# Places for the experts' tokens: 48 tiles of 256 slots and 9 of 128, with the second bias scaled by ScalarE

## The chip, the core and the metric

The program runs on one core of one Trainium2 chip. The metric is the device time of one execution in microseconds. The kernel before was run three times: 1418.8 us is the median, 1416.08 and 1422.6 us are the ends.

## What is computed

The input is an image of two pictures, 56 x 56 positions and 256 channels each, so 6272 tokens. Layer 0 adds a neighbourhood attention (windows of 7 x 7, eight heads). Layer 1 adds a gated linear attention over the tokens in order, and then a mixture of experts, which is the part that the change touches:

```python
xf = _ln_t(t).reshape(-1, 256)                      # 6272 tokens
probs = softmax(xf @ gate_w + gate_b)               # 8 experts
top2_vals, top2_idx = top_k(probs, 2)
cw = zeros((N, 8)).at[arange(N)[:, None], top2_idx].add(top2_vals)
for e in range(8):                                  # W1: 256 x 512, W2: 512 x 256
    h = gelu(xf @ W1[e] + b1[e])
    out += cw[:, e:e+1] * (h @ W2[e] + b2[e])
```

Each token goes to two of the eight experts, so there are 12,544 pairs of token and expert. Everything is float32.

## The kernel before, in words

**Layer 0** (`attend`, `scores`, `context`) comes first. **Layer 1** then walks over 13 steps of 256 positions in both pictures; `before(s)` makes keys, values, queries and coefficients, `attention(s)` the attention itself, and `route(s)` (L1188) the gate of the experts. The order in which these generators are written out is interleaved by hand in `together` (L1517); the framework's scheduler then orders the instructions of each engine, and each engine runs its own in order.

**Routing.** Every expert has a region of rows in the DRAM tensor `xs_d`. `route(s)` counts the tokens of each expert, and writes each normalised token with its index and its weights into the next free row of its two experts, with indirect DMAs that GpSimd issues (L1287, "puts"). `listed(s)` (L1304) keeps a list of tiles: each tile of `SL` = 256 consecutive rows of one expert that is full by now gets the next entry (first row in `l_row`, expert in `l_exp`). After the last step, `listed(NS1)` adds the one partly filled tile that an expert may have at its end. There are `NX` = 56 places in all: 6272 x 2 pairs fill at most that many tiles of 256. A place whose tile doesn't exist points at a spare region. Places 0 to 40 are sure to be known after step 11, place 41 after step 12, and places 42 to 55 after `listed(NS1)`. Before that, eight DMAs on SyncE's queue (L1597) write 256 blank rows behind each expert's last token, so that the unfilled slots of a last tile are harmless.

**Experts.** For each place `k` in order, `experts` (L1493) does this:
- `fetch(k)` (L1369), on SyncE's queue: it loads row and expert into registers, and starts a DMA for the 256 token rows `xg` (272 KB, L1382) and one for the expert's weights `wj` (1154 KB, L1391). A fetch waits for the puts whose rows it reads. Weights and tokens have eight buffers in the last part, where the pool `tw` joins `fw`.
- `gather(k)` (L1394): VectorE takes the token numbers `rowk` and the weights of this expert `cws` out of `xg`; TensorE turns the tokens with four transposes (`pt_g`, L1419) and ScalarE copies them to `xT_g`; GpSimd writes `ye` = second bias times weight, twice 128 x 256 (L1426).
- `hidden(k)` (L1429): eight matmuls (`p_h`, L1436; each float32 matmul runs as two instructions) with 256 moving columns, and four activations with Gelu on ScalarE (L1443).
- `results(k)` (L1447): for each half `u` of 128 slots, four matmuls (`p_y`, L1456), then VectorE adds `p_y` times weight to `ye` (L1463), and GpSimd issues an indirect DMA that adds the 128 rows of `ye` to the rows of `out` (L1466, "adds"). Each add of a tile waits until both adds of the tile before have landed, since two experts can have the same token. `ye` has four buffers (pool `fy`).

`gather(k + 1)` is written out ahead of `results(k)`. In the walk over the steps, expert tiles run beside attention as far as they are known: 39 of them (places 0 to 38) are done when step 12 is routed. The other 17 (places 39 to 55) follow in a last part with nothing beside them, which in the profile begins at 1258.95 us on TensorE.

Of the kernel before, what the change touches and what calls it, by code (L numbers as in the profile page):

```python
# [66 lines left out]
FW = 4  # L67


def size(s):  # L70
    W = min(B1, L - s * B1)
    T = min(P, W)
    return W, T, W // T

# [696 lines left out]
def layer1(tc, t, out, x1_d, xs_d, ident, load, K, plain, lx, last_row, lite):  # L771
# [12 lines left out]
    with ExitStack() as whole:  # L784
# [519 lines left out]
        def listed(s):  # L1304
            last = s == NS1
            lo, hi = sure1(s - 1), NX if last else most1(s)
# [3 lines left out]
            if last:  # L1310
                nc.vector.scalar_tensor_tensor(new, c_prev, float(SL), n_prev, ALU.mult, ALU.is_lt)
# [8 lines left out]
            if hi > lo:  # L1320
# [14 lines left out]
                wide = [P, hi - lo, 2 * NE]  # L1335
                hit = p1.tile(wide, F32, tag="hit", name="hit")
                nc.vector.tensor_tensor(
                    hit,
                    K.c_pos[:, lo:hi].unsqueeze(2).to_broadcast(wide),
                    pos.rearrange("p e i -> p (e i)").unsqueeze(1).to_broadcast(wide),  # L1340
                    ALU.is_equal,
                )
                val = p1.tile(wide, F32, tag="val", name="val")
                add = p1.tile([P, hi - lo], F32, tag="add", name="add")
                for what, of in ((K.l_row, row), (K.l_exp, K.c_exp)):
                    nc.vector.tensor_tensor(
                        val,
                        hit,
                        of.rearrange("p e i -> p (e i)").unsqueeze(1).to_broadcast(wide),
                        ALU.mult,  # L1350
                    )
                    nc.vector.tensor_reduce(add, val, AX.X, ALU.add)
                    nc.vector.tensor_add(what[:, lo:hi], what[:, lo:hi], add)
            state["c"] = c
            known = len(entry)
            now = NX if last else sure1(s)
            if now > known:
                ent = entries.tile([1, 2, NX], I32, tag="ent", name="ent")
                nc.vector.tensor_copy(ent[:, 0, known:now], K.l_row[0:1, known:now])
                nc.vector.tensor_copy(ent[:, 1, known:now], K.l_exp[0:1, known:now])  # L1360
                entry.extend([ent] * (now - known))

        entry, added, puts, stores = [], [], {}, {}
        fetched = {}

        def filled_at(k):
            return next((s for s in range(NS1) if sure1(s) > k), NS1)

        def fetch(k, pool):  # L1369
            known = "the lists hold rows of the regions and experts alone"  # L1370
            row, exp = (
                nc.values_load(
                    entry[k][0:1, n, k : k + 1],
# [5 lines left out]
                for n, top in ((0, NE * RG), (1, NE - 1))  # L1379
# [3 lines left out]
                out=xg, in_=xs_d[bass.ds(row, SL), :].rearrange("(u p) c -> p u c", p=P)  # L1383
# [10 lines left out]
        def gather(k, pool, psum):  # L1394
            xg, wj = fetched[k]
            rowk = fs.tile([P, SL // P], I32, tag="rowk", name="rowk")
            tc.keep_in_program_order(
                nc.vector.tensor_scalar(
                    rowk, xg[:, :, TOK].bitcast(I32), 0.0, float(NB * L + SL - 1), ALU.max, ALU.min
# [4 lines left out]
            for u in range(SL // P):  # L1404
# [4 lines left out]
                        K.l_exp[:, k : k + 1],  # L1409
# [7 lines left out]
            for u in range(SL // P):  # L1417
                for g in range(NG):
                    nc.tensor.transpose(  # L1419
                        pt[:, g, u * P : (u + 1) * P], xg[:, u, g * P : (g + 1) * P], ident  # L1420
                    )
            xT = pool.tile([P, NG, SL], F32, tag="xT_g", name="xT_g")
            nc.scalar.copy(xT, pt)
            y = fy.tile([P, SL // P, C], F32, tag="ye", name="ye")
            for u in range(SL // P):
                nc.gpsimd.tensor_scalar_mul(y[:, u, :], wj[:, WJ - C :], cws[:, u : u + 1])  # L1426
            return xT, cws, rowk, y

        def hidden(xT, wj, pool, psum):  # L1429
            w1 = wj[:, : NG * FF].rearrange("p (k f) -> p k f", k=NG)  # L1430
            b1 = wj[:, NG * FF + NF * C : NG * FF + NF * C + NF]
            hT = pool.tile([P, NF, SL], F32, tag="hT", name="hT")
            for f in range(NF):
                ph = psum.tile([P, SL], F32, tag="mm", name="p_h")
# [12 lines left out]
        def results(k, hT, made, wj, pool, psum):  # L1447
            xT, cws, rowk, y = made
# [4 lines left out]
            for u in range(SL // P):  # L1453
# [27 lines left out]
                if u == 0:  # L1481
                    yield
# [4 lines left out]
        def ask(k):  # L1487
            while use.asked < min(k, NX):
                n = use.asked
                fetch(n, use.w if use.tail is None or (n - use.tail) // FW % 2 else tw)  # L1490
                use.asked += 1

        def experts():  # L1493
            for k in range(NX):
# [6 lines left out]
                if k + 1 < NX:  # L1501
# [83 lines left out]
        behind_ = p1.tile([P, NE], I32, tag="behind", name="behind")  # L1585
# [3 lines left out]
        for e in range(NE):  # L1589
            row = nc.values_load(  # L1590
                behind_[0:1, e : e + 1],
                engines=[mybir.EngineType.SP],
                min_val=e * RG,
                max_val=e * RG + NB * L,
                skip_runtime_bounds_check_because="an expert has at most K.every token",
            )
            put = nc.sync.dma_start(  # L1597
                out=xs_d[bass.ds(row, SL), :].rearrange("(u p) c -> p u c", p=P), in_=empty
            )
            tc.declare_no_dep(put.ins, group="puts", reason="slots behind the last token")  # L1600
# [916 lines left out]
```

## Time and profile before

| what | value |
|---|---|
| time, median of 3 | 1418.8 us |
| time of the profiled execution | 1421.03 us |
| its span in the profile | 1419.2 us |
| granted TensorE clock, mean | 0.938 |
| busy: TensorE, VectorE, GpSimd, ScalarE | 90%, 56%, 41%, 39% |
| adds L1466: number, busy | 112, 179.3 us of GpSimd |
| scalings L1426: number, busy | 112, 126.5 us of GpSimd |
| `p_h` and `p_y` on TensorE | 222.1 us and 214.9 us |
| HBM read and written | 131.55 MB and 50.30 MB |

The span is the time from the first to the last recorded instruction. "Busy" is the time in which an engine ran an instruction; PEld is the loading of weights on TensorE, which runs beside the matmuls. The chain of work that ended last is followed back from the last instruction; it gives one path, and another that is nearly as long doesn't show in it. So the timeline of a single engine has to be read as well, above all GpSimd's, whose queue holds the adds.

### The profile page before, as it was taken

Reading aid. Unit: us, or ns where it says so; the run is one execution under the profiler, and the core shown is the slowest. Engines: PE = TensorE matmul, PEld = TensorE weight load, DVE = VectorE, ACT = ScalarE, POOL = GpSimd, SP = SyncE. Lnnn points to the kernel's source line nnn. Section 1 sums busy time; section 2 is a strip of 40 time slices with the busy share of each in tenths; the row PEclk is TensorE's granted clock in tenths of the full one; section 3 lists DMA queues with packets and bytes.
Section 4 is the critical chain, followed back from the end, with each engine's and each line's share of the span. In section 5 each row is a group of like instructions: output and inputs, shape, how many; then the busy total and the mean of one; then the engine's idle time right before and its main releaser. Section 6 shows DMA issues by size and latency. Waiting matters only on the chain.

```text
span 1419.2 us, 30057 instructions
## 1 busy us (share of the span) xinstructions
PE 1281.3 (90%) x11620; PEld 933.6 (66%) x11620; DVE 799.5 (56%) x2679; ACT 551.3 (39%) x943; POOL 587.9 (41%) x633
## 2 busy tenths in 40 slices
PE   2999989899989997897989999999999999988994
PEld 1567667677845754455666767677676777877883
DVE  6545555565767566767576665657575764331120
ACT  1433434443444232243534445353535344322331
POOL 0222322232321314214172737355554566664774
PEclk9999999999989696887999999999999999999997
DMA  9344454333421011024253536262644546679842
GB/s 290 88 120 144 123 152 123 100 111 113 140 90 40 27 36 62 25 80 151 85 165 93 171 97 202 69 192 83 174 123 125 163 129 195 201 213 373 223 60 34
DMA packets 103036, 183.93 MB, mean 130 GB/s; under 512 B 15666, under 2 KB 86578, under 8 KB 95716
## 3 DMA queue, kind: packets, MB, share of 16 engines
q1 hardware_dynamic: 69844, 128.75, 27.9%
q0 software_dynamic: 29872, 48.12, 14.9%
q10 hardware_dynamic: 3168, 5.05, 1.1%
q8 instruction: 93, 1.52, 0.4%
q14 instruction: 59, 0.48, 0.1%
HBM read 131.55 MB, written 50.30 MB: 128 GB/s over the span
## 4 chain that ended last, share of the span: by engine, by line
PE 49%; DVE 13%; DMA 3%; issue 2%; ACT 2%; POOL 2%; POOLq 0%; DVEq 0%; ACTq 0%
PE p_y L1456 11%; PE p_qkv L917 10%; PE p_h L1436 9%; PE p_out L1170 4%; DMA out<-ye,rowk 3%; PE cx L1152 2%; PE p_u L939 2%; PE cx L1139 2%; PE p_sum L954 2%; PE pt_x L889 2%; DVE am L1101 1%; PE pt_g L1419 1%; PE p_cf L1052 1%; DVE root_a L848 1%; ACT wide L1042 1%
## 5 line engine op out<-in xcount | busy, mean ns | idle before, releaser
L1466 POOL DMA_INDIRECT out<-ye,rowk x112 | 179.3, 1601 | 212.3 <-DMA out<-ye,rowk 44.3
L1436 PE MATMUL p_h<-xT_g,wj 128*128 128x256 f32 x896 | 222.1, 388 | 7.1 <-DVE ye L1463 6.2
L1456 PE MATMUL p_y<-wj,hT 128*128 128x256 f32 x896 | 214.9, 387 | 14.1 <-DVE am L1101 8.0
L1456 PEld LDWEIGHTS p_y<-wj,hT 128*128 128x128 f32 x896 | 166.1, 193 | 43.2 <-DVE am L1101 8.7
L1436 PEld LDWEIGHTS p_h<-xT_g,wj 128*128 128x128 f32 x896 | 163.0, 191 | 34.9 <-DVE ye L1463 6.6
L382 ACT ACTIVATE ex<-ex 98x1024 f32<-98x1024 f32 x98 | 103.6, 1057 | 195.9 <-DVE ex L376 194.6
L1443 ACT ACTIVATE hT<-p_h,wj 128x256 f32<-128x256 f32 x224 | 105.0, 474 | 191.2 <-PE p_h L1436 172.8
L1426 POOL TENSOR_SCALAR ye<-wj,cws 128x256 f32<-128x256 f32 x112 | 126.5, 1309 | 83.4 <-DVE own_e L1406 62.7
L1463 DVE SCALAR_TENSOR_TENSOR ye<-p_y,cws,ye 128x256 f32<-128x256 f32 x112 | 54.0, 482 | 167.9 <-POOL ye L1426 110.4
L376 DVE TENSOR_TENSOR ex<-sc,bias 98x1024 f32<-98x1024 f32 (+1 forms) x112 | 120.2, 1084 | 30.2 <-PE sc L367 27.0
L334 POOL TENSOR_TENSOR xo<-xo,xq 128x256 f32<-128x256 f32 x49 | 36.0, 735 | 225.9 <-DVE xo L328 210.9
L367 PEld LDWEIGHTS sc<-qb,kc 64*98 64x98 f32 x1568 | 94.5, 168 | 51.2 <-issue 27.9
L390 PE MATMUL po<-vw,ex 98*64 98x33 f32 x3136 | 117.6, 230 | 5.0 <-ACT ex L382 2.4
L367 PE MATMUL sc<-qb,kc 64*98 64x128 f32 x1568 | 118.1, 288 | 3.8 <-DVE am L1101 2.2
L390 PEld LDWEIGHTS po<-vw,ex 98*64 98x64 f32 x3136 | 106.2, 144 | 22.8 <-ACT ex L382 4.8
L1287 POOL DMA_INDIRECT xs_d<-xs,rowi x100 | 97.9, 979 | 37.9 <-issue 18.9
L1125 POOL TENSOR_TENSOR zc<-z,blk 128x256 f32<-128x256 f32 x48 | 42.3, 895 | 119.6 <-DVE z L1123 111.6
L494 PE MATMUL pvv<-L_wvT,xs 128*112 128x256 f32 x224 | 60.6, 410 | 14.4 <-DVE top L486 14.4
L1101 DVE TENSOR_TENSOR am<-sc,upto 128x512 f32<-128x512 f32 (+1 forms) x100 | 60.9, 671 | 5.8 <-PE sc L1092 5.8
L336 POOL DMA_DIRECT2D x_d<-xo x98 | 56.6, 579 | 16.6 <-POOL xo L334 14.6
L946 DVE TENSOR_TENSOR pd<-p_u,k 128x512 f32<-128x512 f32 (+1 forms) x26 | 17.2, 661 | 79.1 <-PE pt_gate L1222 64.5
L861 DVE BATCH_NORM_STATS2 st<-x_acc 128x6 f32<-128x256 f32 (+1 forms) x100 | 38.3, 413 | 40.7 <-DMA x_acc<-x_d 40.2
(244 smaller groups left out, 2179.1 us busy)
## 6 DMA issues: line engine op xcount, KB each, us to landing
wj<-in_we SPq DMA_DIRECT2D x56, 1154.0 KB
vw<-v_d SPq DMA_DIRECT2D x196, 101.1 KB
xg<-xs_d SPq DMA_DIRECT2D x56, 272.0 KB
v_d<-values POOLq DMA_DIRECT2D x28, 231.0 KB, 3.2
xq<-in_x SPq DMA_DIRECT2D x98, 64.0 KB
x_d<-xo POOLq DMA_DIRECT2D x98, 64.0 KB, 3.2
x_acc<-x_d SPq DMA_DIRECT2D x24, 256.0 KB
out<-x_acc POOLq DMA_DIRECT2D x24, 256.0 KB, 3.9
```

The lines of the kernel that those rows point to most:

```text
L367: nc.tensor.matmul(at[p][:KN, b, k], lhsT=keys(i, j, k, b, rows, g), rhs=qb[rows, g, :, b, j * QN : (j + 1) * QN], start=True, stop=True,)
L376: nc.vector.tensor_tensor(ex[:KN, of], sc[:KN].rearrange("n p b k h q -> n p b (k h q)"), tables[kind][:KN, g, of].unsqueeze(2).to_broadca ...
L382: nc.scalar.activation(ex[:KN], ex[:KN], AF.Exp)
L390: nc.tensor.matmul(po[b * QN : (b + 1) * QN, hh, :], lhsT=ex[:KN, h // 2, b, k, h % 2, :], rhs=vw[:KN, b, k, hh * (HD + 1) : (hh + 1) * (H ...
L917: nc.tensor.matmul(ps[:, :, :W], lhsT=w[:, kk, g * P : (g + 1) * P], rhs=xT[:, kk, :, :W], start=kk == 0, stop=kk == NG - 1,)
L1101: nc.vector.tensor_tensor(am[:T, h, :, :, :T].rearrange("p b g t -> p (b g) t"), sc[:T, :, :, :T].rearrange("p b g t -> p (b g) t"), K.upt ...
L1287: put = nc.gpsimd.indirect_dma_start(out=xs_d[:, :], out_offset=bass.IndirectOffsetOnAxis(ap=rowi[:T, c, i : i + 1].bitcast(U32), axis=0), ...
L1426: nc.gpsimd.tensor_scalar_mul(y[:, u, :], wj[:, WJ - C :], cws[:, u : u + 1])
L1436: nc.tensor.matmul(ph, lhsT=w1[:, k, f * P : (f + 1) * P], rhs=xT[:, k, :], start=k == 0, stop=k == NG - 1,)
L1443: nc.scalar.activation(hT[:, f, :], ph, AF.Gelu, bias=b1[:, f : f + 1])
L1456: nc.tensor.matmul(py, lhsT=hT[:, f, u * P : (u + 1) * P], rhs=w2[:, f, :], start=f == 0, stop=f == NF - 1,)
L1466: add = nc.gpsimd.indirect_dma_start(out=out[:, :], out_offset=bass.IndirectOffsetOnAxis(ap=rowk[:, u : u + 1].bitcast(U32), axis=0), in_= ...
```

## The change

There are `NP` = 57 places: `NW` = 48 with 256 slots and nine with 128. A partly filled last tile goes into places of 128: one with up to 128 tokens takes one of them, and one with more than 128 takes a place of 256. If fewer than 48 places of 256 are used, the others are spare; if there are more than 48 such tiles (up to `NO` = 52), those above are split over two places of 128 each. `places()` gives the order in which the places are worked on: whole ones 0 to 40, then small and whole ones in turn (small 0, whole 41, small 1, whole 42 and so on to small 6, whole 47), then small 7 and small 8. A small place has half the token rows, transposes, columns of `p_h`, matmuls of `p_y`, and one add in place of two.

The eight blank writes are moved from ahead of `listed(NS1)` into the first fetch that needs them (`blank()`, called ahead of small place 0, the 42nd in order), and their list of rows lives in a pool that stays open. `listed(NS1)` gets a second part (`halved`) of some 20 small VectorE instructions. The scaling of the second bias leaves GpSimd and `gather`; two ScalarE activations in `results` do it, one if the place is small.

The core of the diff (the blank writes are the same eight, moved; `placed` is the old search of positions in a function of its own):

```diff
+NW = 48
+NO = 52
+NP = 57
+def places():
+    order = list(range(NW))
+    first = sure1(NS1 - 2)
+    for n in range(NP - NW):
+        order.insert(min(first + 2 * n, len(order)), NW + n)
+    return order
...
             if last:
-                nc.vector.scalar_tensor_tensor(new, c_prev, float(SL), n_prev, ALU.mult, ALU.is_lt)
+                rest = p2.tile([P, NE], F32, tag="rest", name="rest")
+                nc.vector.scalar_tensor_tensor(rest, c_prev, -float(SL), n_prev, ALU.mult, ALU.add)
+                nc.vector.tensor_single_scalar(new, rest, float(P), ALU.is_gt)
...
+        def halved(large, rest, row):
+            nh = NP - NW
+            over = p1.tile([P, 1], F32, tag="over", name="over")
+            nc.vector.tensor_scalar(over, state["at"], 2.0, -2.0 * NW, ALU.mult, ALU.add)
+            nc.vector.tensor_scalar_max(over, over, 0.0)
+            for n, of in enumerate((K.l_row, K.l_exp)):
+                nc.vector.tensor_copy(
+                    l_half[:, n, : nh - 1].rearrange("p (k u) -> p k u", u=2),
+                    of[:, NW:NO].unsqueeze(2).to_broadcast([P, NO - NW, 2]),
+                )
...
+            few = p1.tile([P, NE], F32, tag="few", name="few")
+            nc.vector.scalar_tensor_tensor(few, rest, 0.0, large, ALU.is_gt, ALU.subtract)
...
+            placed(K.c_pos[:, :nh], at, row[:, :, 0], K.c_e, (l_half[:, 0], l_half[:, 1]))
...
+        def parts(k):
+            return 2 if order[k] < NW else 1
...
         def fetch(k, pool):
+            n = parts(k)
+            if filled_at(k) == NS1 and NS1 not in puts:
+                blank()
...
             get = nc.sync.dma_start(
-                out=xg, in_=xs_d[bass.ds(row, SL), :].rearrange("(u p) c -> p u c", p=P)
+                out=xg[:, :n], in_=xs_d[bass.ds(row, n * P), :].rearrange("(u p) c -> p u c", p=P)
             )
...
-            xT = pool.tile([P, NG, SL], F32, tag="xT_g", name="xT_g")
-            nc.scalar.copy(xT, pt)
-            y = fy.tile([P, SL // P, C], F32, tag="ye", name="ye")
-            for u in range(SL // P):
-                nc.gpsimd.tensor_scalar_mul(y[:, u, :], wj[:, WJ - C :], cws[:, u : u + 1])
-            return xT, cws, rowk, y
+            xT = pool.tile([P, NG, SL], F32, tag="xT_g", name="xT_g")[:, :, : n * P]
+            nc.scalar.copy(xT, pt[:, :, : n * P])
+            return xT, cws, rowk
...
+            y = fy.tile([P, SL // P, C], F32, tag="ye", name="ye")
+            for u in range(parts(k)):
+                nc.scalar.activation(
+                    y[:, u, :], wj[:, WJ - C :], AF.Identity, scale=cws[:, u : u + 1]
+                )
-            for u in range(SL // P):
+            for u in range(parts(k)):
                 py = psum.tile([P, C], F32, tag="mm", name="p_y")
...
         def experts():
-            for k in range(NX):
+            for k in range(NP):
...
-        for e in range(NE):
-            row = nc.values_load(
-                behind_[0:1, e : e + 1],
...
         listed(NS1)
```

## The prediction, made before the result was known

> **What bounds the kernel now.** I read the page's engine line first, then a table of busy time by stretches, then the timelines of GpSimd and TensorE in the last part, and last the waits of TensorE there. TensorE is busy for 90% of the span, which would make every saved matmul a saving. The stretches show where that holds:
>
> ```profile
> PE 1281.3 (90%) x11620; PEld 933.6 (66%) x11620; DVE 799.5 (56%) x2679; ACT 551.3 (39%) x943; POOL 587.9 (41%) x633
> ```
>
> ```profile
> 1100.00:1200.00 100.00, 97.59 (x893) 79.25 (x884) 61.40 (x270) 41.00 (x89) 61.93 (x61) 1.00 0.57 165
> 1200.00:1240.00 40.00, 37.21 (x180) 30.42 (x180) 16.10 (x98) 15.95 (x30) 23.88 (x24) 0.96 0.61 179
> 1240.00:1280.00 40.00, 33.75 (x157) 28.84 (x156) 13.51 (x83) 11.87 (x25) 23.79 (x21) 0.91 0.82 235
> 1280.00:1316.00 36.00, 30.40 (x147) 25.80 (x145) 4.29 (x22) 9.90 (x20) 17.28 (x14) 1.00 1.00 345
> 1316.00:1360.00 44.00, 43.50 (x213) 38.32 (x214) 9.85 (x49) 14.90 (x30) 31.02 (x25) 1.00 0.77 199
> 1360.00:1395.00 35.00, 35.00 (x171) 30.83 (x171) 6.64 (x32) 11.31 (x23) 27.74 (x22) 1.00 0.37 40
> ```
>
> The columns are the stretch, its length, busy us of PE, PEld, DVE, ACT and POOL, then the granted clock, the DMA share and GB/s. Up to 1240 us TensorE sets the pace. From 1240 to 1316 it stands still for 11.9 us while the DMA engines fill up to a share of 1.00. After that TensorE looks like the bound again. GpSimd's timeline (start, length, instruction) says more:
>
> ```profile
> 1281.78 1.58 POOL L1466 DMA_INDIRECT out<-ye,rowk  x1 [0.30 <-issue]
> 1291.74 1.55 POOL L1466 DMA_INDIRECT out<-ye,rowk  x1 [8.38 <-DMA out<-ye,rowk]
> 1293.59 1.55 POOL L1466 DMA_INDIRECT out<-ye,rowk  x1 [0.30 <-issue]
> ...
> 1398.61 1.58 POOL L1466 DMA_INDIRECT out<-ye,rowk  x1 [1.17 <-DVE ye L1463]
> 1400.49 1.59 POOL L1466 DMA_INDIRECT out<-ye,rowk  x1 [0.31 <-issue]
> 1405.17 1.55 POOL L1466 DMA_INDIRECT out<-ye,rowk  x1 [3.09 <-DMA out<-ye,rowk]
> 1407.03 1.55 POOL L1466 DMA_INDIRECT out<-ye,rowk  x1 [0.30 <-issue]
> ```
>
> A tile's two adds go out together, and the next pair waits until they have landed. Counted back from the last, the pair at 1405.17 is place 55, the pair at 1398.61 place 54, and so on without a gap down to place 32 at 1220.91. TensorE's `p_y` of place 54 ended at 1391.95, 6.7 us before its adds; that of place 42 ended at 1298.5, 19 us before. So **the chain of adds lags behind TensorE from 1221 us to the end**, and is the real bound of the last 190 us. TensorE feels it through the stall (its waits there: 6.2 us of `p_h` and 6.1 us of `p_y` on VectorE's `ye`, VectorE in turn 110.4 us on GpSimd's scaling, which stands behind the waiting adds), and the end feels it through the lag.
>
> The chain's prices: from 1353.68 (place 47) to 1405.17 (place 55) are eight cycles in 51.49 us, 6.44 us each where DMA is calm. The second add starts 1.88 us after the first. Where DMA is full (places 36 to 40, starting 1257.16, 1267.55, 1279.89, 1291.74, 1302.41, then 1311.49) a cycle takes 9.1 to 12.3 us. What fills DMA is SyncE: in its timeline the fetch of place 41 starts at 1267.11, when the last route's puts have landed, and eight fetches of 1.43 MB follow by 1289, as far as the eight buffers allow.
>
> [...] 3.90 us from the issue of the add at 1400.49 to landing, and everything else on GpSimd waits behind. [...] an add issued at 1269.48 took 9.67 us beside the fetches. [...] the four transposes below, with 128 x 128 weights and 128 columns, take 0.44 us, 110 ns each. [...]
>
> **The change, part by part.**
>
> Tiles on TensorE. A whole place is one period of this timeline:
>
> ```profile
> 1380.98 3.62 PE L1456 MATMUL p_y<-wj,hT 128*128 128x256 f32 x16
> 1384.44 3.62 PE L1436 MATMUL p_h<-xT_g,wj 128*128 128x256 f32 x16
> 1387.89 0.60 PE L1419 MATMUL pt_g<-ident,xg 128*128 128x128 f32 x4
> 1388.33 3.62 PE L1456 MATMUL p_y<-wj,hT 128*128 128x256 f32 x16
> ```
>
> From start to start 7.35 us: 3.46 + 3.45 + 0.44. A small place has `p_y` 1.73, `pt_g` 0.22, and sixteen `p_h` instructions of 128 columns, which the trace doesn't have. They lie between 0.110 us (the transposes) and 0.216 us (no gain, if the weight loads, 190 ns recorded, couldn't be hidden); I take 0.110, so 1.76. A small place costs 3.71 us (at most 5.41). Eight whole ones less and nine small ones more: 8 x 7.35 - 9 x 3.71 = 25.4 us less on TensorE (10.1 at the other end).
>
> Tiles on the chain of adds. A small place has one add: 6.44 - 1.88 = 4.56 us. Eight cycles less and nine small ones more: 51.5 - 41.0 = **10.5 us less**. This is the smaller number, and it is the one that counts: the chain doesn't end earlier because TensorE does. Whole and small place in turn take 7.35 + 3.71 = 11.06 us of TensorE and 6.44 + 4.56 = 11.0 us of the chain, so the lag that is there when the turns begin stays.
>
> Transfers. The fetches behind 1267 us: 16 weights in place of 15 (+1.15 MB), and tokens of 7 whole and 9 small in place of 15 whole (-0.95 MB): no difference in bytes, but they have some 10 us less. In the full stretch 345 GB/s moved; without the adds' share some 320 reach the fetches, 4.5 us for a whole place and 4.0 for a small one. By the time of the 41st place's add (about 1311) ten have come; `ye` on ScalarE lets TensorE run four places ahead of the landed adds where GpSimd's queue now lets it run three, so buffers come free one place sooner and the backlog ends near 1319 in place of 1308. One more cycle, that of small place 0, falls into it, at 8 to 9 in place of 4 us for landing. Bounds: 0 to +12 us (three places); I take **+2.5 us**, half of one such landing's excess over four plus a little for its neighbour.
>
> Scaling moved to ScalarE. GpSimd loses 112 x 1.31 us (the scaling's row: 126.5 us busy), none of it on the path: in the last part 2.4 us a place lies inside the 4 us of landing, and ahead of 1195 us no wait of TensorE or VectorE ends at it. ScalarE gains 105 activations at [...] 0.59 (the nearest row, Identity with two pointers on 128 x 256, 48 of `xs` at 589 ns mean); I take 0.59, 1.2 us a whole place of 7.35, where ScalarE's own work is four of 0.47 and one of 0.59. A new wait comes with it: the activation waits until the adds four places back have landed, and behind it in ScalarE's queue stand the next Gelus, and behind those TensorE. In the last part that stops TensorE for the chain, which is late already: no cost. In the walk over the steps a place comes every 16 us (66 scalings from 663 to 1195 us) and no add is four places late. There the 0.59 can delay an attention step's exp, tanh or broadcast; TensorE's waits on ScalarE between 600 and 1000 us are 9.8 us in all. Less traffic on GpSimd may give VectorE something back. Bounds -2 to +14 us; I take 0.
>
> List and blanks. Some 20 VectorE instructions of about 0.17 us (the row of `first`, 174 ns) make 3.4 us between 1245 and 1258. They hide in VectorE's 12.9 us of idle time up to 1266.5, and ahead of the fetch that waits until 1267.11 for the puts; without that cover they would cost those 3.4 us of a fetch, not of the chain. The eight blank writes (8.87 us of SyncE from 1245.39) pass no fetch on SyncE's queue: the 41st place was behind them, and small place 0 is. If they did go out after 1267, the fetches would be 9 us later; `p_h` of that place began only at 1282, and its add is due at 1311. I take 0. `l_half`'s memsets and the 57th place's register loads lie under other work.
>
> Sum: -10.5 + 2.5 = -8.0 us. The span becomes 1411.2, the profiled time 1421.03 - 8.0 = 1413.0. That execution was 2.2 us over the median of 1418.8, so I forecast **1410.8 us**.
>
> **Rivals.** (A) The chain of adds bounds, as above: 1410.8, by itself 1405 to 1416. For it: the unbroken lag from 1221 us. (B) TensorE bounds the end after all, and its 25.4 us come through: 1393.4. It needs the adds' landing to shorten or another order of GpSimd's queue in which the lag never starts (it starts when place 32's add stands behind eight puts from 1210.6 to 1220.6); against it, nothing in the diff touches that order on purpose. (C) The backlog of fetches lasts: each place whose add falls into it pays about 4 us more. From 2.6 such places on, the gain is gone; with four it is +16 - 10.5, so 1424.3, slower. For it: small places ask for nearly the same weights in half the time, 8.5 us of fetches in an 11 us turn. Against it: the same load, 0.77 of DMA between 1316 and 1360, left landings near 4.5 us. (D) ScalarE's new work delays one serial step of attention in each of 12 steps by 1.18 us: +14, so 1425. Against it: ScalarE is 41 to 48% busy from 700 to 1200 us.
>
> **How the numbers follow.** A 0.62, B 0.10, C 0.17, D 0.11. The range from 1400 to 1421 holds A and parts of B, C and D. About 0.5% (7.1 us: below 1411.7 or above 1425.9) is what a measurement of this kernel can tell from no change. Faster: two thirds of A and all of B, 0.51. Slower: some of C and of D, 0.07. The same: 0.42.
>
> **What would show it.** Right: in GpSimd's timeline the adds follow one another without a gap to the end, single ones 4.5 us apart, pairs 6.4; TensorE in the last part idles 10 us and more, in short waits; `p_h` of 128 columns takes near 0.11 us from start to start. Wrong: adds that wait for VectorE's `ye` and not for landing (B); cycles of 8 us and more behind 1325 us (C); TensorE's waits on ScalarE ahead of 1200 us grown by 10 us (D).

## The result and the profile after

The median after is 1399.95 us (1395.47 to 1403.46, four runs), that of before in the same comparison 1417.44 us (1412.76 to 1422.6): a ratio of 0.9874 with a 95% interval from 0.9825 to 0.9923. The gain is 17.5 us where 8 were forecast, and the time lies 0.05 us under the range's lower end. The profiled execution of after took 1395.47 us with a span of 1393.7, so it lies 4.5 us under its median, that of before 3.6 over its own: of the 25.5 us between the two spans some 8 are spread between runs.

Cut at the first puts of the first route, of the last but one and at the end, the two spans divide so (us):

| | beginning | walk over the steps | last part | span |
|---|---|---|---|---|
| before | 539.5 | 671.1 | 208.6 | 1419.2 |
| after | 536.9 | 660.8 | 196.0 | 1393.7 |

The last part, which the prediction was about, gives 12.6 us. The walk, where it expected nothing, gives 10.3.

The page's line of TensorE and the others, after:

```profile
PE 1249.2 (90%) x11566; PEld 907.3 (65%) x11566; DVE 788.7 (57%) x2680; ACT 583.6 (42%) x1053; POOL 469.3 (34%) x514
```

TensorE has lost 32 us and its share is still 90%; GpSimd has lost 119 us, ScalarE gained 32. Next the same stretches as shown of before, of after (stretch, length, busy us of PE, PEld, DVE, ACT, POOL, granted clock, DMA share, GB/s):

```profile
1200.00:1240.00 40.00, 29.95 (x146) 24.70 (x145) 7.36 (x40) 15.34 (x34) 18.41 (x15) 0.87 0.68 196
1240.00:1280.00 40.00, 38.48 (x197) 33.63 (x195) 14.64 (x100) 14.40 (x34) 16.21 (x12) 1.00 0.94 302
1280.00:1316.00 36.00, 28.85 (x130) 24.12 (x131) 4.20 (x22) 11.54 (x32) 10.70 (x7) 0.86 0.93 324
1316.00:1360.00 44.00, 42.99 (x236) 36.83 (x235) 8.40 (x44) 17.11 (x48) 17.10 (x12) 1.00 0.57 127
1360.00:1393.70 33.70, 12.56 (x76) 11.15 (x74) 2.13 (x7) 5.60 (x16) 10.80 (x7) 0.75 0.25 30
```

The DMA share is over 0.9 from 1240 to 1316 us (before 0.82, then 1.00). The last row has to be read against the last 33.7 us of before:

```profile
1385.50:1419.20 33.70, 13.36 (x64) 11.41 (x62) 2.11 (x6) 4.38 (x9) 16.35 (x12) 0.74 0.29 34
```

TensorE works 12.6 us there, and 13.4 before. In both kernels its work runs out early and something else ends the kernel. GpSimd's timeline of after shows what (start, length, instruction, in brackets the idle time before it and what ended that):

```profile
1292.49 1.54 POOL L1542 DMA_INDIRECT out<-ye,rowk  x1 [7.36 <-DMA out<-ye,rowk]
1300.68 1.54 POOL L1542 DMA_INDIRECT out<-ye,rowk  x1 [6.65 <-DMA out<-ye,rowk]
...
1360.56 1.54 POOL L1542 DMA_INDIRECT out<-ye,rowk  x1 [2.91 <-DMA out<-ye,rowk]
1362.40 1.54 POOL L1542 DMA_INDIRECT out<-ye,rowk  x1 [0.30 <-issue]
1366.92 1.54 POOL L1542 DMA_INDIRECT out<-ye,rowk  x1 [2.98 <-DMA out<-ye,rowk]
1371.44 1.54 POOL L1542 DMA_INDIRECT out<-ye,rowk  x1 [2.98 <-DMA out<-ye,rowk]
1373.29 1.54 POOL L1542 DMA_INDIRECT out<-ye,rowk  x1 [0.30 <-DVE ye L1539]
1377.82 1.54 POOL L1542 DMA_INDIRECT out<-ye,rowk  x1 [2.98 <-DMA out<-ye,rowk]
1382.11 1.54 POOL L1542 DMA_INDIRECT out<-ye,rowk  x1 [2.75 <-DMA out<-ye,rowk]
```

Whole and small places take turns: a pair goes out 1.84 us apart and the next add follows 4.5 us after its second one, and a single add keeps the next one waiting for 4.5 us as well (1366.92 to 1371.44). Pair and single together take 10.9 us (1360.56 to 1371.44), the forecast was 11.0. The waits of GpSimd behind 1195 us, after, say the same in sum (us, times, longest):

```profile
POOL out L1542 <- DMA out<-ye,rowk: 81.8, 19, 8.5
POOL out L1542 <- DVE ye L1539: 14.8, 4, 7.9
```

And TensorE's timeline of after has the new matmuls:

```profile
1365.15 1.95 PE L1507 MATMUL p_h<-xT_g,wj 128*128 128x128 f32 x16
1366.93 0.38 PE L1492 MATMUL pt_g<-ident,xg 128*128 128x128 f32 x2
1367.15 1.89 PE L1532 MATMUL p_y<-wj,hT 128*128 128x256 f32 x8
1368.88 1.95 PE L1507 MATMUL p_h<-xT_g,wj 128*128 128x128 f32 x16
```

From start to start a small place is 3.73 us (forecast 3.71), and sixteen `p_h` of 128 columns take 1.78 us, 0.111 us each (forecast 0.110).

### The profile page after: what moved, and what is told of

Read it like the earlier page. It is cut to its first block, busy times and chain, and to the rows that moved or that the text cites. A ratio compares the mean times of both kernels' runs of the same rounds, so it can differ in the third digit from the quotient of the medians.

```text
span 1393.7 us, 29855 instructions
## 1 busy us (share of the span) xinstructions
PE 1249.2 (90%) x11566; PEld 907.3 (65%) x11566; DVE 788.7 (57%) x2680; ACT 583.6 (42%) x1053; POOL 469.3 (34%) x514
## 4 chain that ended last, share of the span: by engine, by line
PE 43%; DVE 12%; DMA 4%; issue 3%; ACT 2%; POOL 1%; POOLq 0%; ACTq 0%; DVEq 0%; SPq 0%
PE p_y L1532 11%; PE p_h L1507 9%; PE p_qkv L929 8%; PE p_out L1182 4%; DMA out<-ye,rowk 3%; PE cx L1164 2%; PE p_u L951 2%; PE cx L1151 2%; PE p_sum L966 1%; DVE am L1113 1%; PE pt_x L901 1%; PE p_cf L1064 1%; PE pt_g L1492 1%; ACT wide L1054 1%; DMA out<-x_acc 1%
## 5 line engine op out<-in xcount | busy, mean ns | idle before, releaser
L1542 POOL DMA_INDIRECT out<-ye,rowk x105 | 165.3, 1574 | 357.9 <-DVE ye L1539 100.6
L1532 PE MATMUL p_y<-wj,hT 128*128 128x256 f32 x840 | 206.8, 392 | 25.7 <-ACT hT L1514 19.6
L1507 PE MATMUL p_h<-xT_g,wj 128*128 128x256 f32 (+1 forms) x912 | 209.7, 371 | 2.2 <-DVE ye L1539 1.2
L1532 PEld LDWEIGHTS p_y<-wj,hT 128*128 128x128 f32 x840 | 156.4, 195 | 56.3 <-ACT hT L1514 23.8
L1507 PEld LDWEIGHTS p_h<-xT_g,wj 128*128 128x128 f32 x912 | 155.4, 191 | 27.3 <-issue 6.0
L1514 ACT ACTIVATE hT<-p_h,wj 128x256 f32<-128x256 f32 (+1 forms) x228 | 99.5, 453 | 106.0 <-PE p_h L1507 105.0
L1539 DVE SCALAR_TENSOR_TENSOR ye<-p_y,cws,ye 128x256 f32<-128x256 f32 x105 | 50.4, 480 | 154.8 <-PE p_y L1532 154.7
L1299 POOL DMA_INDIRECT xs_d<-xs,rowi x100 | 98.2, 982 | 70.2 <-DVE first L1341 31.4
L1526 ACT ACTIVATE ye<-wj,cws 128x256 f32<-128x256 f32 x105 | 50.2, 507 | 73.7 <-issue 31.1
L1137 POOL TENSOR_TENSOR zc<-z,blk 128x256 f32<-128x256 f32 x48 | 38.9, 923 | 115.0 <-DVE z L1135 107.0
L1176 ACT COPY cT<-cx 128x256 f32<-128x256 f32 (+1 forms) x50 | 18.3, 366 | 103.1 <-PE cx L1164 102.9
```

Of the source, the lines that this page charges most:

```text
L1299: put = nc.gpsimd.indirect_dma_start(out=xs_d[:, :], out_offset=bass.IndirectOffsetOnAxis(ap=rowi[:T, c, i : i + 1].bitcast(U32), axis=0), ...
L1507: nc.tensor.matmul(ph, lhsT=w1[:, k, f * P : (f + 1) * P], rhs=xT[:, k, :], start=k == 0, stop=k == NG - 1,)
L1514: nc.scalar.activation(hT[:, f, :], ph, AF.Gelu, bias=b1[:, f : f + 1])
L1532: nc.tensor.matmul(py, lhsT=hT[:, f, u * P : (u + 1) * P], rhs=w2[:, f, :], start=f == 0, stop=f == NF - 1,)
L1542: add = nc.gpsimd.indirect_dma_start(out=out[:, :], out_offset=bass.IndirectOffsetOnAxis(ap=rowk[:, u : u + 1].bitcast(U32), axis=0), in_= ...
```

## The experiments

Two questions were open: whether the chain of adds is the bound of the last part, and where the walk's 10 us come from. In each expectation the theories are those that it spells out. Each ratio is to the kernel before, run on the same chip. The chips differ (before took 1417 to 1420 us on most, 1470 on one), so ratios are compared, not times. Every stage below is one profiled execution.

### Tiles alone, scaling alone

`e1_tiles` is after with the scaling as it was: on GpSimd, in `gather`.

```
+            y = fy.tile([P, SL // P, C], F32, tag="ye", name="ye")
+            for u in range(n):
+                nc.gpsimd.tensor_scalar_mul(y[:, u, :], wj[:, WJ - C :], cws[:, u : u + 1])
+            return xT, cws, rowk, y
...
-                nc.scalar.activation(
-                    y[:, u, :], wj[:, WJ - C :], AF.Identity, scale=cws[:, u : u + 1]
-                )
```

> The 57 places in their new order, with the scaling of the second bias left on GpSimd ahead of each tile, as before. Theory 1 (the chain of adds bounds the last part; the small places shorten it by 10.5 us; the move to ScalarE brings little): about 10 us less than before, 1407. Theory 2 (freeing GpSimd of the scaling brings the larger part of the measured 17 us): 5 us less or nothing, 1412 to 1417, and the places of the adds in GpSimd's queue are held up by scalings again.

Measured: ratio 0.9919 [0.9892, 0.9947], 1409.66 us. Last part 200.7 us, 7.9 less than before; walk 668.2, 2.9 less.

`e2_scale` is before with nothing but the scaling moved to ScalarE, into the results.

> The 56 places of 256 as before, with only the scaling moved to ScalarE. Theory 1: within 3 us of before, since whole places on the chain of adds keep their 6.44 us each and the lag stays; TensorE's 12 us of stall between 1240 and 1316 us become shorter without moving the end. Theory 2: 8 to 15 us less than before.

Measured: ratio 0.9924 [0.9894, 0.9954], 1409.14 us, 10.8 us less than before in the same comparison. Last part 206.7 (1.9 less), walk 661.6 (9.5 less). In the last part the tiles give the 8 us that were forecast of them. The scaling, taken at 0, is worth as much as the tiles, and it pays in the walk.

### The small places' adds taken out of the chain

`e3_split` writes the small places' adds into a second tensor, with a chain of its own, so that their results are missing from the output; a copy of the input fills that tensor first.

```
-            before_it = added[-1] if added else []
-            added.append([])
+            small = parts(k) == 1
+            chain_ = added2 if small else added
+            to = out2 if small else out
+            before_it = chain_[-1] if chain_ else []
+            chain_.append([])
```

> The changed kernel with the adds of the nine small places going to a second tensor in DRAM (filled once by a copy of the input), so that they have a chain of their own; what these places compute is left out of the output. Theory 1 (one chain of adds sets the end): the nine cycles of about 5 us leave the chain, and TensorE's work on the last places becomes the bound; about 12 us less than the changed kernel, 1388 where that is 1400. Theory 3 (TensorE or the fetches set the end, the adds only follow them): within 3 us of the changed kernel.

Measured: ratio 0.9902 [0.9869, 0.9935], 1406.58 us. The copy costs at the start (first put at 563.5 us in place of 536.9), which hides the gain in the whole time; the last part took 185.1 us, 10.9 less than after. GpSimd's timeline of `e3_split` near the end:

```profile
1377.26 1.54 POOL L1549 DMA_INDIRECT out<-ye,rowk  x1 [3.86 <-DVE ye L1546]
1379.11 1.54 POOL L1549 DMA_INDIRECT out<-ye,rowk  x1 [0.31 <-DVE own_e L1483]
1382.94 1.54 POOL L1549 DMA_INDIRECT out<-ye,rowk  x1 [2.29 <-DVE own_e L1483]
1388.34 1.54 POOL L1549 DMA_INDIRECT out<-ye,rowk  x1 [3.86 <-DVE ye L1546]
```

The pairs no longer wait for a landing but for VectorE's `ye`, which stands behind TensorE; for the single adds no landing is named either (`own_e` is an earlier instruction of VectorE). A turn of whole and small place is 11.08 us (1377.26 to 1388.34), and TensorE needs 7.35 + 3.73 = 11.08. So TensorE is the bound as soon as the chain is shorter, with only some 11 us to gain.

`e12_split` tried to hide the copy: it goes out from SyncE after steps 1 and 2.

> As e3_split (the adds of the small places go to a second tensor, and what they compute is left out of the output), but the copy that fills it is issued by SyncE behind steps 1 and 2, where DMA is idle for the most part. Theory 1: the last part takes 185 us as in e3_split, and the whole is some 10 us below the changed kernel, ratio 0.980. If the copy still holds something up: the last part 185 us, the ratio higher by what the beginning loses.

Measured: ratio 0.9886 [0.9865, 0.9906], 1400.87 us. Last part 183.5 us, 12.5 less than after, as in `e3_split`; the copy still delays the first put to 552.5. The reading of the last part holds a second time, and a second output bought with a copy is not worth it.

### Fewer fetches ahead, more buffers

`e4_look4` is after with four buffers for the weights of the last part in place of eight.

```
-                fetch(n, use.w if use.tail is None or (n - use.tail) // FW % 2 else tw)
+                fetch(n, use.w if use.tail is None else tw)
```

> The changed kernel with the fetches of the last part going through four buffers in place of eight, so that the burst behind the last route is four places long. Theory 1 with the burst as what makes the adds' landing long: cycles near 1270 to 1310 us fall from 11 to about 7 us and the time by some 10 us, to 1390. If the landing is long for the adds' own sake, or if eight places ahead are needed: the same as the changed kernel, or slower by the waits of TensorE for weights.

Measured: ratio 0.9792 [0.9755, 0.9828], 1391.73 us. Last part 189.5 us, 6.5 less than after. Two of the stretches above, of `e4_look4`:

```profile
1240.00:1280.00 40.00, 40.00 (x204) 35.21 (x203) 16.11 (x109) 16.76 (x40) 16.41 (x12) 1.00 0.94 286
1280.00:1316.00 36.00, 32.79 (x171) 27.51 (x171) 5.61 (x29) 14.14 (x39) 13.91 (x9) 0.95 0.83 231
```

From 1280 to 1316 us DMA moved 231 GB/s where it moved 324 in after, and TensorE worked 32.8 us where it worked 28.9. The cycles of the adds for places 37 to 40 and small place 0 were 7.7, 11.8, 8.5, 6.4 and 5.7 us, in after 7.4, 11.3, 11.9, 10.8 and 8.2. The prefetch asked for weights that nobody needed yet, and paid with the adds that everybody waited for.

`e8_fy6` is after with six buffers for `ye` in place of four, so that ScalarE waits less for landings; `e0_after` is after again, on the same chip.

> The changed kernel with six buffers for the results of tiles in place of four. In the changed kernel TensorE stands still for 10 us near 1210 and for some 10 us more behind 1280, behind ScalarE's scaling that waits for a free one. Theory 1 (the chain of adds sets the end): TensorE's stalls move or go, the time stays within 3 us of the changed kernel, since the adds go out no earlier; it may grow if fetches come earlier into the adds' way. If the stall at 1210 delays the last route: 3 to 8 us less.

> The changed kernel once more, on the chip of the next three runs. All theories: 1397 to 1403 where before is 1418.

Measured: `e8_fy6` 0.9876 [0.9837, 0.9915], 1452.2 us; `e0_after` 0.9871 [0.9837, 0.9904], 1448.98 us; last parts 192.6 and 190.9. ScalarE's waits for `ye` behind 1250 us fell from 48.4 us to 38.1, none of them now put to a landing, and nothing is gained, as forecast. But one long instruction stood in the trace of `e8_fy6`, and it belongs to the next question.

### What the scaling on GpSimd had cost

Two steps of the walk, from 649 to 781 us, show most of it: 132.4 us before, 125.8 in `e2_scale`, 125.0 after. VectorE's timeline of before, in the middle of them:

```profile
731.08 0.16 DVE L850 SCALAR_TENSOR_TENSOR root<-root_a,root 128x4 f32<-128x4 f32 x1
731.28 4.62 DVE L869 SCALAR_TENSOR_TENSOR nm<-mv,root 128x4 f32<-128x4 f32 x1
735.82 0.68 DVE L1074 TENSOR_TENSOR kp<-pt_k,f 128x512 f32<-128x512 f32 x1
```

An operation on four values per partition, 0.16 us as a rule, lasts 4.62 us. No semaphore was waited for: the time is inside the instruction, so no view of waits lists it. GpSimd's timeline of before at that time:

```profile
727.85 1.87 POOL L1426 TENSOR_SCALAR ye<-wj,cws 128x256 f32<-128x256 f32 x2
...
731.30 2.19 POOL L1193 DMA_DIRECT2D out<-x_acc  x2
732.90 2.96 POOL L902 TENSOR_TENSOR x_acc<-x_acc,bo 128x1024 f32<-128x1024 f32 x1
```

The instruction stands still from the issue of the stores (731.30) to the end of the addition of the output bias (732.90 + 2.96 = 735.86), and goes on at 735.9. Two stretches of before have the consequence:

```profile
730.00:736.00 6.00, 3.88 (x46) 2.82 (x45) 5.76 (x9) 0.55 (x3) 5.60 (x4) 0.99 0.83 226
736.00:742.00 6.00, 5.36 (x48) 4.34 (x49) 3.63 (x12) 4.32 (x9) 4.51 (x5) 0.50 1.02 356
```

TensorE works 3.88 of 6 us and stands still for 2.77 us at a stretch (up to 736.64), and in the next 6 us its clock reads 0.50.

What this costs is read from the whole step. These are the second of the two steps in before and in `e2_scale`:

```profile
715.30:781.10 65.80, 61.58 (x459) 44.37 (x459) 41.90 (x166) 28.39 (x54) 32.89 (x31) 0.95 0.47 139
710.70:772.80 62.10, 58.94 (x459) 42.30 (x459) 37.69 (x169) 31.84 (x62) 25.37 (x23) 1.00 0.51 147
```

The same 459 matmuls take 2.6 us less of TensorE's time at full clock, and it idles 1.1 us less: 3.7 us. The first of the two steps (from 648.7 and 647.0 us on) gives 2.9 us more, 1.9 of them TensorE's time at a clock of 0.86 and 0.88; there VectorE's longest instruction on four values is 3.17 us before and 2.33 in `e2_scale`. In the second step of `e2_scale` the chain of small operations was through a few tenths of a microsecond earlier; VectorE's timeline there:

```profile
726.45 0.16 DVE L869 SCALAR_TENSOR_TENSOR nm<-mv,root 128x4 f32<-128x4 f32 x1
...
728.21 2.48 DVE L1101 TENSOR_TENSOR am<-sc,upto 128x512 f32<-128x512 f32 x4 [0.99 <-PE sc L1092]
730.74 0.69 DVE L1398 TENSOR_SCALAR rowk<-xg 128x2 int32<-128x2 int32 x1
```

and GpSimd's of `e2_scale`:

```profile
726.86 2.12 POOL L1193 DMA_DIRECT2D out<-x_acc  x2
728.38 3.02 POOL L902 TENSOR_TENSOR x_acc<-x_acc,bo 128x1024 f32<-128x1024 f32 x1
```

`nm` begins 0.41 us ahead of the stores, and is done. Under the addition VectorE multiplies `am` out of PSUM at 0.62 us each; only `rowk` of 128 x 2, all in SBUF, ends with the addition and not sooner (0.69 us).

In these two timelines the instructions that are held have all their inputs in SBUF (`nm` of before two, 4.62 us; `rowk` of `e2_scale` one, 0.69 us), and `am`, at 0.62 us each, has one in PSUM. The recorded starts don't tell when: `nm` of before begins 0.02 us ahead of the stores and 1.62 us ahead of the addition and is held all the same. Why is not shown.

`e5_bias_dve` tests whether the addition has to be on GpSimd for it: before, with the addition (L902) on VectorE.

```
-            nc.gpsimd.tensor_tensor(
+            nc.vector.tensor_tensor(
                 x[:T, :, :nj, :],
```

> The kernel before, scaling on GpSimd and 56 places, with only the addition of the output bias to x (GpSimd, 128 x 1024, 13 times 2.6 us) done by VectorE. Theory C (the scalings push that addition behind, and while it runs VectorE's small instructions in SBUF stand still; the one of 4.62 us in the step from 715 to 781 us is the cost that moving the scaling removed): VectorE's instructions of over 1 us there are gone, the two steps between 649 and 781 us take some 126 in place of 132 us, and the time is 5 to 8 us less than before. Theory S (it is the scaling's own place in GpSimd's queue, ahead of puts and adds): the same as before, within 2 us, or slower by the 1.1 us a step that VectorE gets more.

Measured: ratio 0.9863 [0.9827, 0.99], 1448.75 us, on the chip with 1469.99 us before: 21.2 us less, where 5 to 8 were expected. The two steps took 124.8 us and have no long small instruction, though the scaling is still on GpSimd. So the hold goes with the addition on GpSimd, and without it the two steps are short. The rest of the 21 us can't be put to these two steps. On this chip other steps are held too: in `e0_after`, with the scaling on ScalarE, an instruction on four values stands for 1.9 to 4.5 us in each of the six steps from 772 us on, and the first five of them take 72 to 76 us, in `e5_bias_dve` 69 to 72. Before was not profiled there. Nor does the run tell the hold from the addition's own 2.6 us a step, which leave GpSimd's queue as well.

The first put came late (547.9 us, against 536.1 for after on the same chip); I put that down to VectorE, which may be short of time in the first steps, but no run tests it. So the later kernels move the addition only for `s > 2`. And `e8_fy6` shows the converse, the scaling on ScalarE and the hold all the same. VectorE there, the small instruction this time with one input, in SBUF:

```profile
725.41 5.00 DVE L853 TENSOR_SCALAR root_a<-ve 128x4 int32<-128x4 int32 x1
```

and GpSimd of `e8_fy6`:

```profile
725.88 2.13 POOL L1205 DMA_DIRECT2D out<-x_acc  x2
727.40 2.98 POOL L914 TENSOR_TENSOR x_acc<-x_acc,bo 128x1024 f32<-128x1024 f32 x1
```

The two steps took 132.8 us in that run and 126.3 in `e0_after`. So the hold comes with the scaling on ScalarE as well. What decides is not shown: the held instruction began 0.02 us ahead of the stores in before and 0.47 us in `e8_fy6`, the one that went through 0.41 us in `e2_scale`. The part of the scaling is seen in the first of the two steps of before: the addition begins at 664.94, when a pair of scalings (663.12, 1.85 us) ends, and VectorE's instruction of 3.17 us, begun at 664.14, ends with it. In the second step its part is not shown.

`e7_both` puts the addition on VectorE and takes four weight buffers, on after.

> The changed kernel with four buffers for the fetches of the last part (measured before at 1391.7) and the addition of the output bias on VectorE. Theory C: the remaining stalls of 2 to 3 us of VectorE's small instructions, one in each step, are gone as well; most of them are hidden now, so 0 to 4 us less: 1388 to 1392. Theory S: 1392 or a few us more.

Measured: ratio 0.9652 [0.9607, 0.9698], 1417.1 us, 31.9 less than `e0_after` on the same chip, where 8 to 12 less than after were expected. The forecast was made from another chip; on this one the five steps from 772 us on take 69 to 71 us here and 72 to 76 in `e0_after`.

`e10_tiles_bias` is `e1_tiles`, `e11_after_bias` is after, both with the addition on VectorE for `s > 2`.

> The 57 places with the scaling on GpSimd (as in e1_tiles, ratio 0.992), and the output bias added by VectorE from step 3 on, so that no GpSimd addition holds VectorE's small instructions there. Theory C: the steps from 649 to 781 us fall to some 125 us and the ratio to about 0.983 or below; beside e11_after_bias it loses only what the scaling costs in the last part, 2 to 4 us. Theory S (the scaling on GpSimd costs by itself): it stays 8 us or more behind e11_after_bias.

> The changed kernel with the output bias added by VectorE from step 3 on. Theory C: the stall that the move of the scaling avoided is gone already, so this brings less than it brings e10_tiles_bias: ratio 0.980 to 0.987 on a chip whose steps run at full clock, down to 0.975 on a slower one.

Measured: 0.9821 [0.9796, 0.9845], 1393.29 us, and 0.9785 [0.9761, 0.981], 1388.27 us. Neither has a hold in those steps, and each is about 1% under its partner (0.9919 and 0.9874). If the hold were all, the two would now be alike. They differ by 0.36%, 5 us, in medians, with a slight overlap of the intervals: more than the 2 to 4 us of the one theory, less than the 8 of the other. In the profiles, which lie 10.3 us apart, 2.8 are in the steps from 649 to 781 us (126.5 and 123.7), most of them in the second. That step of `e10_tiles_bias`, then of `e11_after_bias`:

```profile
703.80:768.80 65.00, 61.95 (x459) 43.74 (x459) 38.13 (x167) 28.50 (x54) 31.35 (x31) 0.95 0.49 140
```

```profile
702.00:764.90 62.90, 60.56 (x459) 43.22 (x459) 37.96 (x170) 31.84 (x62) 23.99 (x22) 0.97 0.50 145
```

The same 459 matmuls, 2.1 us apart, GpSimd at 31.4 and 24.0 us. TensorE's timelines differ in one wait, `e10_tiles_bias` first:

```profile
736.23 3.68 PE L929 MATMUL p_qkv<-xT_a,L_wvT 128*128 128x512 f32 x4 [2.38 <-DVE z L1135]
733.90 1.98 PE L929 MATMUL p_qkv<-xT_a,L_wvT 128*128 128x512 f32 x4 [1.57 <-DVE z L1135]
```

VectorE's `z` stands behind an instruction that waits for the next `x_acc` from DRAM, 11.2 us in the one and 10.4 in the other; that load is held on SyncE's queue until the step's stores of `x_acc` have landed, 10.0 and 9.0 us. Behind the longer gap the four matmuls run slower (3.68 us; the clock from 733.8 to 739.8 us reads 0.72), behind the shorter one they don't (1.98 us, 1.00). TensorE's busy time makes 1.4 of the 2.1 us, its idle time the rest.

So about half of what the scaling was worth in these steps (126.5 - 123.7 = 2.8 against 130.2 - 125.0 = 5.2 with the addition on GpSimd) is not this hold. As far as these two traces show, most of it is a later load with a slower clock behind it; no run tests that. Why the stores land later with the scaling on GpSimd stays open, and so do the 0.8 us of the first step.

### Whose time it was, and which place in the queue

The scaling was moved in two ways at once: to another engine and from `gather` to the results. `e13_pool_late` is after with the scaling on GpSimd, but in the results.

```
-                nc.scalar.activation(
-                    y[:, u, :], wj[:, WJ - C :], AF.Identity, scale=cws[:, u : u + 1]
-                )
+                nc.gpsimd.tensor_scalar_mul(y[:, u, :], wj[:, WJ - C :], cws[:, u : u + 1])
```

> The changed kernel with the scaling back on GpSimd, but written out where ScalarE does it (in results, not in gather), and so later in GpSimd's queue. If the place in the queue cost the time: as the changed kernel, ratio 0.987, the two steps from 649 to 781 us in 125. If GpSimd's time costs it, wherever it stands: as e1_tiles, 0.992, those steps in 130.

Measured: ratio 0.9943 [0.9927, 0.9959], 1410.62 us; walk 668.0, as in `e1_tiles`, the two steps 130.2. VectorE of `e13_pool_late`:

```profile
724.86 4.62 DVE L860 TENSOR_TENSOR root_a<-root 128x4 f32<-128x4 f32 x1
```

The hold is back. It was GpSimd's time that mattered and not the place. `e14_dve` gives the scaling to VectorE (`nc.vector.tensor_scalar_mul`) at the same place.

> The changed kernel with the scaling on VectorE in place of ScalarE. If it is GpSimd's relief that counts: as the changed kernel, 0.987, or better by the free ScalarE. If ScalarE's part were needed (its wait for a free buffer throttles TensorE): VectorE now holds that wait, with the routing behind it, and the last part is longer than 196 us.

Measured: ratio 0.9931 [0.9905, 0.9957], 1409.13 us. The walk is 663.0, near after's 660.8, although a hold is there, 4.54 us at 722.63. The relief of GpSimd thus counts even where VectorE pays for it. And the hold alone is not the price: the two steps take 126.8 us, 3.4 less than in `e13_pool_late` with a hold as long. The second of them, of `e14_dve`:

```profile
706.70:770.20 63.50, 58.96 (x459) 42.33 (x459) 44.91 (x176) 28.22 (x54) 25.28 (x24) 1.00 0.50 143
```

TensorE stopped for 2.46 us behind the hold, 2.82 in `e13_pool_late`, and the clock stayed at 1.00 (58.96 us busy); there TensorE was busy for 61.71 us, as in before (61.58 us at a clock of 0.95). With the hold but without the slow clock the step is 2.1 us longer than after's 61.4. The length of the gap alone doesn't tell which it will be: 2.38 us were enough in `e10_tiles_bias`.

The last part is 205.9, 9.9 worse than after. VectorE's waits behind 1195 us, in `e14_dve`:

```profile
DVE ye L1526 <- issue: 77.9, 13, 10.3
DVE ye L1526 <- DMA out<-ye,rowk: 28.0, 5, 9.8
```

Now VectorE holds the wait for a free `ye` (for most of it the profile names no releaser, for 28.0 us a landing), and its other work, the last route's list too, stands behind it. Of the two, ScalarE is the better engine to hold that wait.

`e15_held` tried to bring the delay back into after, with two needless scalings on GpSimd ahead of the addition.

```
+            for _ in range(2):
+                spare = p1.tile([P, C], F32, tag="spare", name="spare")
+                nc.gpsimd.tensor_scalar_mul(spare[:T], x[:T, 0, 0, :], K.wgb[:T])
```

> The changed kernel with two useless GpSimd scalings of 128 x 256 (1.9 us together) ahead of each addition of the output bias on GpSimd. Theory C (that addition, pushed behind by GpSimd work, meets VectorE's small serial instructions): a stall of VectorE of over 3 us comes back in the step from 715 to 781 us and the two steps take 130 us or more; ratio 0.991 to 0.994. If it is not that: the same as the changed kernel.

Measured: ratio 0.986 [0.9831, 0.9888], 1398.96 us, as after. No small instruction in that step lasted over 1.3 us, but the two scalings did not run ahead of that step's addition either (none in GpSimd's timeline from 711 to 735 us). So the delay was not brought back, and the run says nothing of what it would do.

### What follows from it all

`e9_best` is after with the addition on VectorE for `s > 2` and four weight buffers.

> Both: four buffers for the last fetches and the output bias on VectorE from step 3 on. If the two gains add up: ratio 0.97 or below, 6 us or more below e11_after_bias.

Measured: ratio 0.975 [0.9731, 0.9768], 1383.46 us; it is faster than before by 2.5%, and than after by over 1% if ratios of two chips are compared. It lies 4.8 us below `e11_after_bias`, so the two gains didn't add up in full. In the last part the buffers' gain doesn't show here: 194.8 us against 194.5 in `e11_after_bias`, where `e4_look4` had 189.5 against 196.0. From the last route's first put to the end it is 146.8 against 149.0, but the stage ahead of that took 2.4 longer. Why is not shown.

## Why the prediction was half right

**The chain of adds bounds the last part: right, and shown.** The adds follow one another's landing to the end, TensorE idles 40.9 us of the last part (196.0 less 155.1 busy, before 32.7), and with the small adds out of the chain (`e3_split`, `e12_split`) the part shortens by 10.9 and 12.5 us; near the end of `e3_split` the waits go over to VectorE's `ye`. Rival B, TensorE's own saving coming through, is out for this kernel.

**Tiles and backlog, -10.5 + 2.5 = -8.0: right in sum, in part by luck.** Tiles alone took 7.9 us off the last part. The terms measured 4.5 us for a single add where DMA is calm, 6.3 to 6.5 for a pair, 0.111 us for the new `p_h`. But the sum describes the chain from the adds of the 42nd place in order to the end. That took 107.7 us before (from 1311.49), 101.2 after (from 1292.49) and 101.8 in `e1_tiles`: 6.5 and 5.9 us less. The other 2.0 us of `e1_tiles` were gained ahead of these adds, where the prediction has no term, and 6.1 of after's 12.6.

The backlog was under-priced. The first four cycles of small places took 8.2, 7.5, 6.2 and 5.2 us, over 4.5 by 9.1 us in sum, while the six cycles of places 41 to 46 of before, at the same point, were over 6.44 by 3.5. The difference is 5.6 us, the forecast was 2.5. Rival C's mechanism was there, at half its price for each place. `e4_look4` shows that the backlog was a choice: with half the prefetch 6.5 us of it go. Differences of 2 or 3 us shouldn't be leant on, since kernels that are alike in the last part differ by as much in single profiles: it took 196.0 us in after and 198.8 in `e15_held`.

**"Scaling moved to ScalarE ... I take 0": this step failed.** Alone it is worth 10.8 us (`e2_scale`), against a bound of -2, and on top of the tiles some 6 (0.9919 to 0.9874). The reason given was that "ahead of 1195 us no wait of TensorE or VectorE ends at it". True, and not enough: GpSimd's scalings can push its later instructions into the time of others (1.85 us ahead of the addition at 664.94 us of before; 126.5 us in all; the 1.31 us is the mean of one, but two overlap, 1.87 us a pair). One case is shown: the addition of the output bias falls on VectorE's norm and holds it for 4.6 us, TensorE stops for 2.8 us and runs on with a slow clock (0.50 over 6 us), and the step is 3.7 us longer than in `e2_scale`, most of that by the clock. The other case is the load of `x_acc` in `e10_tiles_bias`. Both lie in the two steps that gave 6.6 of the walk's 9.5 us in `e2_scale`. The sign stood there, "Less traffic on GpSimd may give VectorE something back", but without a place and a price. Both could have been had from the trace of before. Its answer for the line of `nm`:

```profile
L869 DVE SCALAR_TENSOR_TENSOR nm<-mv,root x26: 138/161/4620, 400.0 to 1214.3; 128x4 f32<-128x4 f32 x24, 64x2 f32<-64x2 f32 x2
```

Shortest, median, longest in ns. A longest of 29 medians, for an instruction that moves next to nothing, was the thing to ask about.

**Where the rest lies.** From `e1_tiles` to after the last part lost a further 4.7 us in the profiles, 2.8 of them ahead of the last route's first put (50.6 to 47.8), the rest behind it; the other steps of the walk lose up to 0.8 us each. These are seen, not explained, and the 4.7 us are not far above the 2.8 by which like kernels differ. They are what stays open of the scaling's effect, together with the reason for the later stores.

**The rest of the list at 0:** nothing contradicts it. Rival D, ScalarE's new work on a serial step, didn't come about: the walk got shorter. The activation took 507 ns in the mean, 105 times; the 590 that I took were too many.

## What to carry to other kernels

The serial chain of dependent adds counted in landings here: halving a tile saved the second issue (1.9 us) and not the landing (4.5 us from a single add to the next), whatever it saved on TensorE. With such a chain, take its bytes off the way, or take the add out of the chain. When an engine is relieved, its waits are not the whole list of those who profit: for each small instruction of a serial chain compare the longest duration with the median, and look at what the other engines ran beside the longest (here 4.62 us against 0.16, beside an addition of 128 x 1024 on GpSimd). And a prefetch deeper than needed can cost where something that everybody waits for goes the same way (6.5 us of the last part in `e4_look4`, nothing in that of `e9_best`).

## What the runs showed of the hardware

A VectorE operation on 128 x 4 values in SBUF, 0.16 us as a rule, was held for 4.54 to 5.00 us beside a GpSimd addition of 128 x 1024 and went on when that ended, in before, `e1_tiles`, `e8_fy6`, `e13_pool_late` and `e14_dve`. In four of the five it had begun within 0.03 us of the stores that GpSimd issues ahead of the addition, in `e8_fy6` 0.47 us ahead of them. A 128 x 512 multiplication with one input in PSUM ran beside the same addition at 0.62 us (`e2_scale`). A gap of 2.77 us in TensorE's work was followed by 6 us at a clock of 0.50 (before), one of 2.46 us by none (`e14_dve`), and with one of 2.38 us the clock over 6 us read 0.72 (`e10_tiles_bias`). With two copies of the input within DRAM, early in the kernel, the first put came 16 and 27 us later (`e12_split`, `e3_split`).
